# Fifth attention of a graph network: more weighing on the scalar engine, the norms' scalings moved to other passes, and the last two node tiles normalised one by one

## The chip, the cores and the metric

The kernel runs on one core of a Trainium2 chip. The core has a matrix engine (TensorE, PE), a vector engine (VectorE, DVE), a scalar engine (ScalarE, ACT), a general engine (GpSimd, POOL) and a queue that only issues transfers (SyncE, SP). [...]

The metric is the device time of one launch in microseconds (us), the median of several runs. The profile is one further execution, recorded by the hardware; its span runs from the first to the last instruction.

## The reference, cut to what matters

Four layers work on x, 8 batches x 2048 nodes x 64 features, over one graph. Each layer ends in `x = layernorm(x + layer(x))`. The change touches the last attention of the last layer (the fifth attention of the whole) and what follows it:

```python
def _gat_layer(h, mask, b):
    scores = jnp.einsum('...nd,...md->...nm', h, h)
    scores = jnp.where(mask, scores, NEG)
    attn = jax.nn.softmax(scores, axis=-1)
    return jnp.einsum('...nm,...md->...nd', attn, h) + b
...
out2 = _gat_layer(h2, mask[None], bo)
z2 = jax.nn.leaky_relu(out2, negative_slope=0.2)
mu = jnp.mean(z2, axis=-1, keepdims=True)
var = jnp.mean(jnp.square(z2 - mu), axis=-1, keepdims=True)
out = (z2 - mu) * jax.lax.rsqrt(var + LN_EPS) * gamma + beta
...
x = _layernorm(x + out, axis=-1)
```

So after the attention each node gets: a leaky ReLU, a first normalisation, a product with gamma, the addition of x (beta is already in x), and a second normalisation, which gives the result.

## The kernel before

The graph is sparse, so the kernel doesn't compute all scores. The 2048 nodes are 16 node tiles of 128. The edges of a node tile lie in 3 slots x 4 groups; a **unit** is one slot and two groups, so a node tile has 6 units (`PER`), and the stage has 96. Node tiles are treated in pairs, of 12 units.

For one unit the steps are:

- `fetch`: POOL starts two gathers, which bring the rows of the neighbours (`hs`, 128 edges x 8 batches x 64 features, twice) from a table in memory. Nine such buffers; units are fetched five passes ahead.
- `expand`: PE copies each node's own row to its edges (`pe`), by six matrix products with `selTb`, a 0/1 matrix in bf16.
- `score`: DVE multiplies `pe` and `hs` (`pr`, L1155) and sums over the features (`sc`, L1160); ACT takes the exponential into `w` (L1162), and for two units of three once more into `w_ps` in PSUM (L1164).
- `weigh_act` and `weigh`: the row of each edge is multiplied by its weight (`wx`). Of three units, POOL does the first whole (128x1024, L1176), ACT (eight activations of 128x64, L1171) and DVE (128x512, L1176) do half each of the second, and DVE does the third whole (128x1024, L1176). DVE reads the weights from `w_ps`.
- `add_up`: PE sums the weighed rows and the weights into the nodes (`po` L1188, `pd` L1190), with `self_`, a 0/1 matrix.

For one node tile follow `invert` (DVE, the reciprocal of `pd`, L1193), `divide` (ACT, eight activations, L1199), `leaky` (DVE, L1202), `take_stats` (DVE: `bn_stats` L137, then twelve small operations, L140 to L143, among them three Newton steps for the inverse root), `normalise` (ACT, eight activations, L151), `residual` (POOL: product with gamma L1215, addition of x L1216), again `take_stats`, and `store` (ACT scales, SP stores). `take_stats` does both tiles of a pair in one chain. `start` (SP and ACT) brings `hi` and makes `selTb` and `self_` for the next node tile.

The order is written out by hand (`manual_schedule`): one loop over passes u. Pass u does, in this order: fetch of unit u+5; score of unit u+1 (with `invert` between its product and its sum where a tile has ended); `weigh_act` of u-1; expand of u+2; `weigh` of u-1; add_up of u-2; then the work of whole tiles that a dictionary `after` gives by its offset; and, where u % 6 is 3, `start` of the next tile. An entry at offset j falls into the pass whose number, within its pair of twelve, is (j + 11) modulo 12. So before the change: `divide` of the first tile in pass 9 and its `leaky` in 10; `divide` of the second in 3, its `leaky` and the pair's statistics in 4; scalings in 6 and 7; gamma and x on POOL in 7 and 8; second statistics in 9; last scalings and stores in 10 and 0. `start` is in 3 and 9.

The buffers that matter: `pe` 2, `hs` 9, `wx` 4, `w` 5, `z` 6. The tile `w_ps` is one PSUM tile, and a read of any part of it waits for the last write to any part.

Of the kernel before, what the change touches and what calls it, by code (L numbers as in the profile page):

```python
# [27 lines left out]
AF = mybir.ActivationFunctionType  # L28
ALU = mybir.AluOpType
# [19 lines left out]
def kernel(ctx: ExitStack, tc: tile.TileContext, ins: dict, out: bass.AP):  # L49
    nc = tc.nc  # L50
    x, adj = ins["x"], ins["adj"]
    B, N, D = x.shape
    NT = N // P
# [26 lines left out]
    def rows(name, src, pool):  # L80

        n = src.shape[0]
        t = pool.tile([P, n], F32, name=name)
        nc.sync.dma_start(t, src.unsqueeze(0).to_broadcast([P, n]))
        return t

    def over(v, shape):

        for _ in shape[1:-1]:
            v = v.unsqueeze(1)  # L90
        return v.to_broadcast(shape)

    def along(v):

        return v.unsqueeze(len(v.shape)).to_broadcast([*v.shape, D])
# [25 lines left out]
    def inv_sqrt(y, v, t):  # L121

        nc.vector.scalar_tensor_tensor(y.bitcast(I32), v.bitcast(I32), -0.5, guess.to_broadcast(v.shape),
                                       op0=ALU.mult, op1=ALU.add)
        for _ in range(3):
            nc.vector.tensor_tensor(t, y, y, ALU.mult)
            nc.vector.scalar_tensor_tensor(t, t, -0.5, v, op0=ALU.mult, op1=ALU.mult)
            nc.vector.scalar_tensor_tensor(y, t, 1.5, y, op0=ALU.add, op1=ALU.mult)

    def norm_stats(chunks):  # L130

        n = len(chunks)
        st = small.tile([P, n, NP, 6], F32, name=f"st{n}")

        for c, v in enumerate(chunks):
            for a in range(NP):
                nc.vector.bn_stats(st[:, c, a], v[:, 2 * a:2 * a + 2, :].rearrange("p b d -> p d b"))  # L137
        triples = st.rearrange("p n a (k m) -> p (n a k) m", m=3)
        var, rstd, tmp, nmr = (small.tile([P, n * B], F32, name=f"ln_{k}{n}") for k in "vrtm")
        nc.vector.scalar_tensor_tensor(var, triples[:, :, 2], 1.0 / D, eps.to_broadcast(var.shape),  # L140
                                       op0=ALU.mult, op1=ALU.add)
        inv_sqrt(rstd, var, tmp)
        nc.vector.scalar_tensor_tensor(nmr, triples[:, :, 1], -1.0, rstd, op0=ALU.mult, op1=ALU.mult)  # L143
        return rstd, nmr

    def normed(chunks, stats):
        rstd, nmr = stats
        for c, v in enumerate(chunks):
            for b in range(B):
                k = c * B + b  # L150
                nc.scalar.activation(v[:, b], v[:, b], AF.Identity, scale=rstd[:, k:k + 1], bias=nmr[:, k:k + 1])  # L151
# [10 lines left out]
    X = main.tile([P, NT, B, D], F32, name="X")  # L162
# [97 lines left out]
    def node_products(t0, wk, ps):  # L260
# [26 lines left out]
        for q, ph in enumerate(held):  # L287
# [26 lines left out]
                                   op0=ALU.is_equal, op1=ALU.mult)  # L314
# [8 lines left out]
    for it in range(NT):  # L323
# [18 lines left out]
        for k in range(0, SL, 8):  # L342
            nc.vector.max(nbr[:, k:k + 8], topf)
            if k + 8 < SL:
# [19 lines left out]
                                       op0=ALU.is_le, op1=ALU.mult, saturate=False)  # L364
# [27 lines left out]
    held, zs, stats = {}, {}, {}  # L392
# [28 lines left out]
    def weigh(it):  # L421
        hs, self_, w, wm = held[it]
        po = ps_o.tile([P, BD], F32, name="po")
        pd = ps_w.tile([P, NG, B], F32, name="pd")
        for s in range(GS):
            own = slice(s * NG, (s + 1) * NG)
            wx = hs[:, own].rearrange("p g b d -> p (g b) d")
            nc.vector.tensor_tensor(wx, wx, along(w[:, own].rearrange("p g b -> p (g b)")), ALU.mult)  # L428
            nc.tensor.matmul(pd, self_[:, s], wm[:, own], start=(s == 0), stop=(s == GS - 1))
            for g in range(NG):  # L430
                nodes = slice(g * GN, (g + 1) * GN)
                nc.tensor.matmul(po[nodes], self_[:, s, nodes], hs[:, s * NG + g].rearrange("p b d -> p (b d)"),
                                 start=(s == 0), stop=(s == GS - 1))
        held[it] = po, pd
# [66 lines left out]
    with ExitStack() as l1:  # L501
# [115 lines left out]
        n = 0  # L617
# [94 lines left out]
    with ExitStack() as l2:  # L712
# [65 lines left out]
        def take_stats(st, k, v):  # L778
            for a in range(NP):
                nc.vector.bn_stats(st[:, k, a], v[:, 2 * a:2 * a + 2, :].rearrange("p b d -> p d b"))  # L780
# [76 lines left out]
        with tc.manual_schedule(engines=engines):  # L857
# [4 lines left out]
            n = 0  # L862
# [37 lines left out]
    with early, ExitStack() as heads:  # L900
# [6 lines left out]
        Us, os, xss, xsTs, ws, pos, h2s, zs, dTs = ({} for _ in range(9))  # L907
# [172 lines left out]
        with tc.manual_schedule(engines=engines):  # L1080
# [8 lines left out]
            for k in range(len(steps)):  # L1089
# [4 lines left out]
                it = steps[k][0]  # L1094
# [11 lines left out]
    with ExitStack() as fifth:  # L1106
# [10 lines left out]
        g3 = rows("g3", ins["L3_gnn_gamma"], fp)  # L1117
# [16 lines left out]
        units = [(it, s, g) for it in range(NT) for s in range(GS) for g in range(0, NG, 2)]  # L1134
        hss, pes, ws, wxs, zs, stats, sums = ({} for _ in range(7))
# [30 lines left out]

        def weigh_act(u):
            wxs[u] = fk.tile([P, 2, B, D], F32, name="wx", bufs=4)
            if u % 3 == 1:
                for b in range(B):  # L1170
                    nc.scalar.activation(wxs[u][:, 0, b], hss[u][:, 0, b], AF.Copy, scale=ws[u][:, 0, b:b + 1])  # L1171

        def weigh(u):
            eng, w = (nc.vector, w_ps[:, u % 3]) if u % 3 else (nc.gpsimd, ws[u])
            ks = slice(1, 2) if u % 3 == 1 else slice(0, 2)
            eng.tensor_tensor(wxs[u][:, ks].rearrange("p k b d -> p (k b) d"),  # L1176
                              hss[u][:, ks].rearrange("p k b d -> p (k b) d"),
                              along(w[:, ks].rearrange("p k b -> p (k b)")), ALU.mult)
# [23 lines left out]
            nc.vector.scalar_tensor_tensor(zs[it], zs[it], 0.2, zs[it], op0=ALU.mult, op1=ALU.max)  # L1202


        def take_stats(it):
            stats[it] = norm_stats([zs[it], zs[it + 1]])

        def normalise(it):
            rstd, nmr = stats[it - it % 2]
            own = slice(it % 2 * B, it % 2 * B + B)  # L1210
            normed([zs[it]], (rstd[:, own], nmr[:, own]))

        def residual(it):
            z = zs[it]
            nc.gpsimd.tensor_tensor(z, z, over(g3, z.shape), ALU.mult)  # L1215
            nc.gpsimd.tensor_tensor(z, z, X[:, it], ALU.add)  # L1216

        def store(it):
            normalise(it)
            nc.sync.dma_start(out[:, it * P:(it + 1) * P, :].rearrange("b p d -> p b d"), zs[it])  # L1220
# [1 line left out]


        after = {-2: [(divide, 0)], -1: [(leaky, 0)], 4: [(divide, 1)], 5: [(leaky, 1), (take_stats, 0)],
                 7: [(normalise, 0)], 8: [(residual, 0), (normalise, 1)], 9: [(residual, 1)], 10: [(take_stats, 0)],
                 11: [(store, 0)], 13: [(store, 1)]}
        PER = GS * NG // 2
        AHEAD = 5
        last = len(units) - 1
        with tc.manual_schedule(engines=engines):  # L1230
            for u in range(AHEAD):
                fetch(u)
            start(0)
            expand(0)
            expand(1)
            score(0, [])
            for u in range(len(units) + 14):
                if u + AHEAD <= last:
                    fetch(u + AHEAD)
                done, r = divmod(u - 2, PER)  # L1240
                ended = [(invert, done - 1)] if r == 0 and 1 <= done <= NT else []
                if u + 1 <= last:
                    score(u + 1, ended)
                else:
                    for f, a in ended:
                        f(a)
                if 1 <= u <= last + 1:
                    weigh_act(u - 1)
                if u + 2 <= last:
                    expand(u + 2)  # L1250
                if 1 <= u <= last + 1:
                    weigh(u - 1)
                if 2 <= u <= last + 2:
                    add_up(u - 2)
                for j, fs in after.items():
                    for k in (u - j - 2 * PER + 1,):
                        if k % (2 * PER) == 0 and 0 <= k < len(units):
                            for f, n in fs:
                                f(k // PER + n)
                if u % PER == 3 and u // PER + 1 < NT:  # L1260
                    start(u // PER + 1)

# [29 lines left out]
    with tc.If(bad > 0), ExitStack() as anyway:  # L1292
# [12 lines left out]
        X = main.tile([P, NT, B, D], F32, name="X")  # L1305
# [13 lines left out]
        with tc.tile_pool(name="adjp", bufs=3) as ap_, tc.tile_pool(name="adjps", bufs=4, space=PSUM) as aps:  # L1319
            for it in range(NT):  # L1320
# [15 lines left out]
                own = ap_.tile([P, P], F32, name="own")  # L1336
# [8 lines left out]
            for c in range(NCH):  # L1345
                pr = aps.tile([1, TPC, P], F32, name="pt")
                for k in range(TPC):
                    it = c * TPC + k
# [32 lines left out]
        with ExitStack() as l0:  # L1381
# [71 lines left out]
            for b in range(B):  # L1453
                p, k = divmod(b, 2)
# [8 lines left out]
                for ih in range(2):  # L1463
                    acc = [pa.tile([P, CW], F32, name="acc") for _ in range(2)]
                    for jt in range(NT):
                        w = pp.tile([P, HW], F32, name="w")
                        nc.vector.tensor_scalar(w, F[:, ih * HW:(ih + 1) * HW], Cj[:, jt, b:b + 1], Aj[:, jt, b:b + 1],
                                                op0=ALU.mult, op1=ALU.max)
                        nc.vector.scalar_tensor_tensor(w, MT[:, jt, ih * HW:(ih + 1) * HW], 0.0, w,
                                                       op0=ALU.is_equal, op1=ALU.mult)  # L1470
# [11 lines left out]
                if k == 1:  # L1482
                    for c in range(NCH):
# [6 lines left out]
                        v = wk.tile([P, TPC, P], F32, name="v", tag="t2")  # L1490
# [17 lines left out]
        with ExitStack() as l1:  # L1508
# [15 lines left out]
            for t in range(NT):  # L1524
# [7 lines left out]
                for h in range(2):  # L1532
                    hs = slice(h * HB * D, (h + 1) * HB * D)
                    f = R[:, t, h, 1]
# [99 lines left out]
        with ExitStack() as l3:  # L1634
# [44 lines left out]
            bias = wp.tile([D, HN + 1], F32, name="bias")  # L1679
# [3 lines left out]
            g3 = rows("g3", ins["L3_gnn_gamma"], wp)  # L1683
# [107 lines left out]
            units = [(b, h) for b in range(B) for h in range(HN + 1)]  # L1791
# [37 lines left out]
```

## Time and profile before

| what | value |
|---|---|
| timed runs, median of 3 | 2254.24 us (2251.59 to 2255.79) |
| profiled execution, its own time | 2154.42 us |
| span of the profiled execution | 2152.5 us |
| mean granted TensorE clock over the span | 0.791 |
| granted TensorE clock in the fifth attention | 0.50 |
| fifth attention, first gather to the end of the span | 1720.3 to 2152.5 us |
| busy in the span: PE, DVE, ACT, POOL | 1554.6, 1413.8, 992.9, 1068.2 us |

The profiled execution took 100 us less than the timed median. Times inside the kernel come from the profiled execution.

A line of the timeline has the start in us from the start of the span, the duration in us, the engine, the line of the code, the operation, what it writes and reads, how many instructions are merged, and in brackets the idle time before it with what ended it. A line of the windows has the stretch, its length, and for each engine the busy time and (in brackets) the number of instructions; then TensorE's granted clock, the mean busy share of the DMA engines, and GB/s. `DMA_INDIRECT` on POOL is the issue of one gather, not its transfer.

### The profile page before, as it was taken

The numbers are of one execution on the slowest core, as the hardware profiler recorded it, in microseconds if no ns is written. First come the engines' busy times: TensorE is split into PE (matmuls) and PEld (weight loads), VectorE is DVE, ScalarE is ACT, GpSimd is POOL, SyncE is SP. The second block draws the span as 40 slices with busy tenths as digits, with TensorE's granted clock in tenths as the row PEclk, the third lists the DMA queues.
The fourth block names the chain that finished last, engine by engine and source line by source line (L and its number), as shares of the span: only waits on it lengthen the run. The fifth ranks groups of instructions, "written<-read, shape, count | busy, mean of one in ns | idle before, by whom it ended". The sixth has DMA issues, their size and how long they took to land.

```text
span 2152.5 us, 35828 instructions
## 1 busy us (share of the span) xinstructions
PE 1554.6 (72%) x13538; PEld 879.8 (41%) x13574; DVE 1413.8 (66%) x2986; ACT 992.9 (46%) x2336; POOL 1068.2 (50%) x992
## 2 busy tenths in 40 slices
PE   3662445434899979475599998998999578888872
PEld 3552112111333354121477777777777422222210
DVE  6888488885655574445345555555555379999995
ACT  4552134448523242636445444444444235555555
POOL 0000777734645446342345455455454387777662
PEclk9965566656999999788699999999999655555555
DMA  6321666631278725443323233233233065555540
GB/s 195 132 98 63 208 204 206 206 101 60 99 270 294 256 69 155 129 122 93 108 71 110 83 98 110 84 98 109 85 99 92 34 200 153 160 159 156 156 125 21
DMA packets 134244, 283.70 MB, mean 132 GB/s; under 512 B 64144, under 2 KB 66704, under 8 KB 131984
## 3 DMA queue, kind: packets, MB, share of 16 engines
q0 software_dynamic: 64896, 217.10, 33.3%
q1 hardware_dynamic: 52528, 60.03, 8.4%
q10 hardware_dynamic: 16640, 4.20, 0.9%
q8 instruction: 109, 1.79, 0.3%
q14 instruction: 71, 0.58, 0.1%
HBM read 245.35 MB, written 35.91 MB: 131 GB/s over the span
## 4 chain that ended last, share of the span: by engine, by line
PE 35%; DVE 18%; ACT 10%; issue 5%; POOL 2%; DMA 2%; SPq 1%; ACTq 0%; POOLq 0%; DVEq 0%
PE pscore L968 9%; PE pa L556 6%; DVE w L977 4%; PE pa L867 3%; ACT w L971 3%; PE pm L1030 3%; PE po L994 3%; PE pt L953 2%; DVE pr L1155 2%; ACT z L786 2%; PE pm L920 2%; PE pa L608 2%; PE po L1188 2%; ACT z L151 2%; DVE sc L1160 2%
## 5 line engine op out<-in xcount | busy, mean ns | idle before, releaser
L977 DVE SCALAR_TENSOR_TENSOR w<-w,Sel 128x512 f32<-128x512 f32 (+1 forms) x192 | 178.9, 959 | 234.8 <-ACT w L971 234.2
L186 POOL DMA_INDIRECT hs<-htab,src x192 | 183.7, 957 | 267.2 <-PE pe L408 206.0
L186 POOL DMA_INDIRECT xs<-xtab,src x192 | 205.4, 1070 | 123.0 <-issue 93.6
L556 PE MATMUL pa<-R,ET 128*128 128x512 bf16 x841 | 196.5, 388 | 52.9 <-POOL R L544 34.0
L186 POOL DMA_INDIRECT hs<-ktab,src x192 | 186.3, 971 | 54.9 <-issue 42.1
L971 ACT ACTIVATE w<-pscore 128x1024 f32<-128x1024 f32 x128 | 131.0, 1023 | 164.3 <-PE pscore L968 163.7
L968 PE MATMUL pscore<-U,xsT 64*128 64x64 f32 (+1 forms) x3072 | 203.6, 280 | 3.3 <-DVE U L931 3.3
L968 PEld LDWEIGHTS pscore<-U,xsT 64*128 64x128 f32 x3072 | 184.0, 190 | 29.0 <-issue 21.5
L1038 POOL TENSOR_TENSOR h<-h,h2h 128x512 f32<-128x512 f32 x48 | 60.9, 1269 | 250.1 <-DVE h2h L1032 250.1
L955 ACT COPY xsT<-pt 128x512 f32<-128x512 f32 x192 | 112.1, 584 | 141.4 <-PE pt L953 141.4
L1150 PE MATMUL pe<-hi,selTb 32*128 32x512 bf16 x576 | 138.8, 619 | 50.5 <-DVE pr L1155 30.3
L151 ACT ACTIVATE X<-X,ln_m,ln_r 128x64 f32<-128x64 f32 x256 | 87.2, 428 | 172.0 <-DVE ln_m L143 172.0
L556 PEld LDWEIGHTS <-ET 128*128 128x128 fp8e4 x864 | 84.1, 99 | 174.2 <-issue 82.5
L994 PE MATMUL po<-w,xs 128*64 128x64 f32 (+1 forms) x3072 | 143.8, 243 | 2.0 <-DVE w L977 1.8
L953 PE MATMUL pt<-ident,xs 128*128 128x128 f32 x768 | 128.1, 290 | 8.0 <-DMA xs<-xtab,src 5.4
L994 PEld LDWEIGHTS po<-w,xs 128*64 128x64 f32 x3072 | 119.5, 137 | 34.9 <-issue 29.3
L1155 DVE TENSOR_TENSOR pr<-pe,hs 128x1024 f32<-128x1024 f32 x96 | 116.8, 1217 | 14.4 <-DMA hs<-ktab,src 10.5
L186 POOL DMA_INDIRECT rs<-ytab,src x84 | 80.7, 961 | 83.6 <-PE pa L847 60.5
L1160 DVE TENSOR_REDUCE sc<-pr 128x16 f32<-128x1024 f32 x96 | 117.1, 1220 | 2.9
L1162 ACT ACTIVATE w<-sc,shift 128x16 f32<-128x16 f32 x96 | 29.3, 305 | 191.3 <-DVE sc L1160 187.3
L186 POOL DMA_INDIRECT rs<-rtab,src x84 | 79.6, 948 | 72.9 <-PE pa L608 52.8
L428 DVE TENSOR_TENSOR hs<-hs,w 128x2048 f32<-128x2048 f32 x48 | 106.7, 2277 | 0.5 <-ACT w L418 0.5
(577 smaller groups left out, 3307.9 us busy)
## 6 DMA issues: line engine op xcount, KB each, us to landing
at<-in_adj SPq DMA_DIRECT2D x16, 1024.0 KB
rtab<-r SPq DMA_DIRECT2D x16, 512.0 KB
ptab<-hp SPq DMA_DIRECT2D x16, 384.0 KB
hi<-ptab SPq DMA_DIRECT2D x16, 384.0 KB
X<-in_x ACTq DMA_DIRECT2D x16, 256.0 KB
htab<-H SPq DMA_DIRECT2D x16, 256.0 KB
ytab<-y SPq DMA_DIRECT2D x16, 256.0 KB
ktab<-hb SPq DMA_DIRECT2D x16, 256.0 KB
```

What stands on the lines that cost most here:

```text
L151: nc.scalar.activation(v[:, b], v[:, b], AF.Identity, scale=rstd[:, k:k + 1], bias=nmr[:, k:k + 1])
L186: nc.gpsimd.indirect_dma_start(out=dst, out_offset=None, in_=table[:, :], in_offset=bass.IndirectOffsetOnAxis(ap=src[:, it, s, g:g + 1], a ...
L556: nc.tensor.matmul(po[h].rearrange("p a f -> p (a f)"), ET[:, jt, it * P:(it + 1) * P], R[:, jt, q, h].rearrange("p a f -> p (a f)"), star ...
L953: nc.tensor.transpose(pt[:, p], xss[k][n][:, p * P:(p + 1) * P], ident)
L955: nc.scalar.copy(xsT, pt)
L968: nc.tensor.matmul(pscore[:, k_, f0:f0 + HN * ni].rearrange("p (h i) -> p h i", i=ni), xsTs[k][t][half, p], Us[it][half, p, :, i0:i0 + ni] ...
L971: nc.scalar.activation(w.rearrange("p t k a h i -> p k t (a h i)"), pscore.rearrange("p k (t m) -> p k t m", t=n), AF.Exp)
L977: nc.vector.scalar_tensor_tensor(wt, wt, 3.0e38, edge, op0=ALU.min, op1=ALU.mult)
L994: nc.tensor.matmul(po[half, p, :, i0:i0 + ni], xss[k][t][:, f0:f0 + D], ws[k][:, t, k_, p], start=(s == 0 and p == 0), stop=(last and p == ...
L1150: nc.tensor.matmul(pe[:, k].rearrange("p b d -> p (b d)"), selTb[nodes, s * P:(s + 1) * P], hi[nodes, q], start=(q == 0), stop=(q == 2))
L1155: nc.vector.tensor_tensor(pr.rearrange("p k b d -> p (k b d)"), pes[u].rearrange("p k b d -> p (k b d)"), hss[u].rearrange("p k b d -> p ( ...
L1160: nc.vector.tensor_reduce(sc, pr, AX.X, ALU.add)
```

## The change

Five things are altered.

- ACT now does half of the weighing of the third unit of three as well, and DVE the other half. DVE has no whole weighing left.
- The entries of `after` move. First scalings: passes 7 and 10 (before: 6 and 7). Gamma and x of the first tile: pass 8; gamma of the second: pass 11; x of the second and the second statistics: pass 0 (before: statistics in 9). Last scalings and stores: passes 1 and 4 (before: 10 and 0).
- Adding x is on DVE for the second tile of each pair, on POOL for the first.
- The last two node tiles (14 and 15) don't go through `after`, but through a second dictionary, `alone`, with statistics of one tile each; their offset j is counted from the last unit of the tile itself, so that tile 14 has `divide` and `leaky` in pass 92, statistics and scaling in 93, gamma, x and second statistics in 94, and the store in 95; tile 15 the same in 98 to 101. Their scalings are shared, four batches on ACT and four on DVE, and gamma and x are on DVE.
- The loop ends seven passes earlier.

In a pass, entries of `after` come before those of `alone`.

```diff
         def weigh_act(u):
             wxs[u] = fk.tile([P, 2, B, D], F32, name="wx", bufs=4)
-            if u % 3 == 1:
+            if u % 3:
                 for b in range(B):
                     nc.scalar.activation(wxs[u][:, 0, b], hss[u][:, 0, b], AF.Copy, scale=ws[u][:, 0, b:b + 1])
 
         def weigh(u):
             eng, w = (nc.vector, w_ps[:, u % 3]) if u % 3 else (nc.gpsimd, ws[u])
-            ks = slice(1, 2) if u % 3 == 1 else slice(0, 2)
+            ks = slice(1, 2) if u % 3 else slice(0, 2)
...
+        PAIRED = NT - 2
+
         def take_stats(it):
-            stats[it] = norm_stats([zs[it], zs[it + 1]])
+            stats[it] = norm_stats([zs[it], zs[it + 1]] if it < PAIRED else [zs[it]])
 
         def normalise(it):
-            rstd, nmr = stats[it - it % 2]
-            own = slice(it % 2 * B, it % 2 * B + B)
-            normed([zs[it]], (rstd[:, own], nmr[:, own]))
-
-        def residual(it):
+            if it < PAIRED:
+                rstd, nmr = stats[it - it % 2]
+                own = slice(it % 2 * B, it % 2 * B + B)
+                normed([zs[it]], (rstd[:, own], nmr[:, own]))
+                return
+            rstd, nmr = stats[it]
+            for b in range(B):
+                v, r, n = zs[it][:, b], rstd[:, b:b + 1], nmr[:, b:b + 1]
+                if b % 2:
+                    nc.scalar.activation(v, v, AF.Identity, scale=r, bias=n)
+                else:
+                    nc.vector.tensor_scalar(v, v, r, n, op0=ALU.mult, op1=ALU.add)
+
+        def with_gamma(it):
             z = zs[it]
-            nc.gpsimd.tensor_tensor(z, z, over(g3, z.shape), ALU.mult)
-            nc.gpsimd.tensor_tensor(z, z, X[:, it], ALU.add)
+            eng = nc.gpsimd if it < PAIRED else nc.vector
+            eng.tensor_tensor(z, z, over(g3, z.shape), ALU.mult)
+
+        def with_x(it):
+            z = zs[it]
+            eng = nc.vector if it % 2 or it >= PAIRED else nc.gpsimd
+            eng.tensor_tensor(z, z, X[:, it], ALU.add)
...
         after = {-2: [(divide, 0)], -1: [(leaky, 0)], 4: [(divide, 1)], 5: [(leaky, 1), (take_stats, 0)],
-                 7: [(normalise, 0)], 8: [(residual, 0), (normalise, 1)], 9: [(residual, 1)], 10: [(take_stats, 0)],
-                 11: [(store, 0)], 13: [(store, 1)]}
+                 8: [(normalise, 0)], 9: [(with_gamma, 0), (with_x, 0)], 11: [(normalise, 1)], 12: [(with_gamma, 1)],
+                 13: [(with_x, 1), (take_stats, 0)], 14: [(store, 0)], 17: [(store, 1)]}
+
+        alone = {3: [divide, leaky], 4: [take_stats, normalise], 5: [with_gamma, with_x, take_stats], 6: [store]}
...
-            for u in range(len(units) + 14):
+            for u in range(len(units) + 7):
...
                 for j, fs in after.items():
-                    for k in (u - j - 2 * PER + 1,):
-                        if k % (2 * PER) == 0 and 0 <= k < len(units):
-                            for f, n in fs:
-                                f(k // PER + n)
+                    k = u - j - 2 * PER + 1
+                    if k % (2 * PER) == 0 and 0 <= k < PAIRED * PER:
+                        for f, n in fs:
+                            f(k // PER + n)
+                for j, fs in alone.items():
+                    k = u - j - PER + 1
+                    if k % PER == 0 and PAIRED * PER <= k < len(units):
+                        for f in fs:
+                            f(k // PER)
```

## The prediction

> **What bounds the kernel now.** I read, in this order: the page (engines, 40 slices), the windows of the fifth attention, its groups of instructions by form, the timeline of one period, and the timeline of the end. The fifth attention runs from about 1720 us to the end of the span. It repeats every two node tiles, that is every 12 passes of the loop; passes and units are counted from 0 within a pair (in the end: from the start of the stage), and pass u scores unit u+1, weighs u-1 and expands u+2:
>
> ```profile
> core 0: us, PE busy (x) PEld busy (x) DVE busy (x) ACT busy (x) POOL busy (x), PEclk, DMA share, GB/s
> 1852.99:1903.16 50.17, 40.31 (x170) 10.53 (x168) 46.61 (x77) 28.15 (x105) 36.05 (x33) 0.50 0.54 153
> 1903.16:1953.31 50.15, 40.32 (x170) 10.52 (x168) 46.59 (x78) 28.16 (x105) 36.03 (x33) 0.50 0.54 152
> ```
>
> The windows run from one reciprocal (L1193) to the same one a pair later. DVE works 46.6 of 50.15 us; ACT looks free for 22. What the engines do around pass 9 of a pair:
>
> ```profile
> 1857.62 0.26 ACT L1164 ACTIVATE w_ps<-sc,shift 128x16 f32<-128x16 f32 x1
> 1857.82 1.72 ACT L1199 ACTIVATE z<-po,recs 128x64 f32<-128x64 f32 x8
> 1857.91 1.22 DVE L1176 TENSOR_TENSOR wx<-hs,w_ps 128x1024 f32<-128x1024 f32 x1 [0.60 <-ACT w_ps L1164]
> ...
> 1859.39 0.56 ACT L1128 ACTIVATE selTb<-SelT 128x384 bf16<-128x384 fp8e4 x1
> ...
> 1860.01 1.46 PE L1150 MATMUL pe<-hi,selTb 32*128 32x512 bf16 x6 [0.63 <-ACT selTb L1128]
> ...
> 1862.71 0.96 POOL L186 DMA_INDIRECT hs<-ktab,src  x1 [0.30 <-issue]
> ...
> 1863.04 2.59 DVE L143 SCALAR_TENSOR_TENSOR ln_m<-st,ln_r 128x16 f32<-128x16 f32 x1
> ...
> 1863.68 1.91 POOL L1176 TENSOR_TENSOR wx<-hs,w 128x1024 f32<-128x1024 f32 x1
> 1865.56 1.21 DVE L1155 TENSOR_TENSOR pr<-pe,hs 128x1024 f32<-128x1024 f32 x1
> ...
> 1871.40 2.00 ACT L1171 ACTIVATE wx<-hs,w 128x64 f32<-128x64 f32 x8
> ```
>
> Three things to see. PE gets selTb only after ACT's eight divisions; DVE doesn't feel it, because it is in the statistics of this place. L143 takes 2.59 us where its twin at 1892.34 takes 0.17, and ends with POOL's weighing. And DVE waits 0.60 for w_ps.
>
> Spacings on DVE, from the same timeline: product to sum 1.25, sum to next 1.14, half weighing 0.60, whole weighing 1.14, a weighing behind w_ps 0.68 later. Three units are 3 x 2.39 + 0.60 + 0.68 + 1.14 = 9.58. A pair: 4 x 9.58 + two leaky at 0.60 + two statistics at 4.15 + the stretched L143 2.41 = 50.2, the period. So DVE's order is the bound, and PE (3.32 a unit, 40) is next.
>
> [...] The trace agrees: L143, and one leaky of 1.61 us (median 0.68) that ends 0.56 after POOL's weighing. [...] 332 ns with one pointer, 426 with two, eight in 2.00 us, so the next starts after 1.91.
>
> **The change part by part, for a pair.**
> *Weighing.* DVE's four whole weighings become halves: -4 x 0.54 = -2.2. ACT gets 4 x 8 activations, 1.91 us each time, behind w_ps and ahead of what else is queued in that pass. In passes 3 and 9 these are the divisions, then selTb and self_. So leaky in passes 4 and 10 waits: in pass 4 before, the divisions ended at 1885.79 and leaky began at 1887.69; now 1887.70 against 1887.14. +0.6 in pass 4.
> *Passes 9 to 11.* From w_ps (0.29 ahead of the weighing of unit 8): weighing by ACT at 0.20, divisions 1.91 later, selTb 1.57 later, 0.56 for it, 0.06 to PE, 1.50 until the product may start: product 0 at 5.5 after that weighing. DVE would be there after 0.60 + 1.25 + 1.14 + 0.60 = 3.6: +1.9 (0.6 of it in front of leaky). Before, 6.5 us of statistics lay here; they move to pass 0. PE's next expansion comes 1.39 + 1.92 = 3.31 later, DVE's 2.99: +0.3.
> *Adding x.* One of two on DVE: +0.6 at leaky's spacing (128x512, both inputs in SBUF). POOL loses 1.3, and isn't the bound.
> *Statistics moved.* The old collision goes: -2.41. Is there a new one? Count from the sum of unit 8. ACT: exp 1.32 later, 0.21 and 0.20, eight scalings 2.75, end at 4.5. POOL waits there with gamma for tile 0, then, at spacings of the trace: gamma +0.08, x 1.35, four gathers 1.42 + 1.30 + 1.26 + 1.27, weighing 0.97, gathers 2.07 + 1.30, gamma 0.98, gathers 1.41 + 1.30 + 1.26 + 1.27, weighing of unit 0 after 0.97: at 22.7, to 24.6. [...] DVE: to the weighing of unit 8 7.2, product 0 at 12.7, product 1 at 16.0, then 1.25 + 1.82 + 0.60 + adding x 0.60 + eight bn_stats 1.69: the twelve small operations (2.5 in all) begin at 22.0. So they meet POOL's weighing at their first or second, wait until 24.6, and ten are left, 2.1: +2.2 (2.6 if all twelve wait). Bounds: 0 if they miss it, 2.6.
> Scalings in other units: ACT's longest row now (scalings, exp, eight weighings) ends 0.2 before the exp of unit 4 is due; nothing added. SP's stores now alternate with hi; hi leaves behind unit 11's expansion, 4 us ahead of selTb: nothing.
> Sum: 50.15 - 2.2 + 0.6 + 1.9 + 0.3 + 0.6 - 2.4 + 2.2 = 51.2, some +1.1 a pair (1.2 unrounded). Six pairs between passes 20 and 92: +7. Before pass 20, where PE is the bound and only selTb's delay shows: +0.7.
>
> **The end.** Product 93 starts at 2102.54, the span ends 50.0 later. After, from that product: ACT has scalings until 3.3, exp, eight weighings until 5.4, divisions of tile 14 until 7.1; leaky 14 stands directly behind in DVE's queue, ahead of product 94, and waits for them and for POOL's weighing of unit 93 (end 7.9): done 8.5. Product and sum 94, weighing, statistics (four bn_stats 0.85, twelve small 2.5) 15.4; four tensor_scalar 128x64 aren't in the trace: [...] 15.9. Sum 95 at 17.2, gamma and x 1.4, second statistics with 1.2 lost to POOL's gamma: 24.2. Two weighings, scalings, x and the paired statistics: 30.7. ACT then scales tile 12 first, 33.4, and divides tile 15, 35.1. Leaky 35.9, statistics 39.2, scalings on both engines 40.7, gamma and x 42.2, statistics 45.5, scalings 47.0, last store 4.4 (as before): 51.4. Normalising the last tile alone shortens what follows its leaky from 26.0 (2126.5 to 2152.5) to 15.5, but the stalls ahead eat it: +1.4 (-4 to +5).
>
> Together 7 + 0.7 + 1.4 = +9, with the unrounded +1.2 9.5: profiled execution 2154.42 to 2164. The timed median, 2254.24, is 100 us above the profiled execution; I assume that lies in stages where TensorE's granted clock is above the 0.50 of this one, so the same difference holds: 2263.7.
>
> **Rivals.** *Cover holds:* ACT's idle 22 us really take the weighings, and the new place meets no POOL weighing. Then DVE's own sum, 50.15 - 2.2 + 0.6 - 2.4 = 46.2, -3.9 a pair, six pairs and the end's -1: 2230. For it: the busy shares. Against: the fixed queue order. It decides if selTb comes within 3.6 us of the weighing of unit 8 and leaky finds its divisions done. *Collision missed:* the small operations pass POOL by 2.6 us on either side; 6 x 2.2 less: 2250. My two paths meet within 0.1, so an error of 0.5 doesn't miss. *Second collision:* leaky of pass 10 starts 0.6 ahead of POOL's weighing of unit 9; if it is late it waits 2.6, of which the next collision gives half back: +1 to +2 a pair, 2270 to 2276.
>
> **How the numbers follow.** Forecast 0.53 (own range 2256 to 2271), cover holds 0.17, collision missed 0.15, second collision 0.15. A measurement of this kernel tells about 0.2% (4.5 us) from no change. Slower: forecast and second collision, less a little, 0.66; same: most of collision missed and the edge of the forecast, 0.15; faster 0.19. Range 2247 to 2275: it leaves out cover holds and a rest.
>
> **What would show it.** In the new profile: period 51.2; DVE's product 0 of each pair waiting more than 1 us for PE, which waits for selTb; leaky waiting for ACT's divisions; L140 or L123 stretched beyond 2 us, L143 at 0.17; leaky 14 waiting some 4 us. A period under 49, a product 0 without wait, or no stretched small operation would prove me wrong.

## The result and the profile after

The changed kernel took 2264.57 us (median of 6 runs, 2260.22 to 2269.09), the kernel before, timed beside it, 2254.74 (6 runs, 2251.22 to 2256.64). The ratio is 1.0048, with a 95% interval of 1.0031 to 1.0065: slower by some 10 us (by the interval 7 to 15).

The profiled execution of after took 2262.87 us, its span 2260.9; that of before had 2152.5. Most of this difference is not the change's: the reciprocal in pass 8, the first with which the two can be compared, comes at 1758.34 in before and at 1854.82 in after, 96 us later, ahead of all that was altered. From there to the end of the span before needs 394.1 us and after 406.1, so the stage itself got 12.0 us longer. Of these 1.3 lie between the reciprocals of passes 8 and 20, 8.6 in the six pairs from 20 to 92, and 2.1 behind 92.

The windows of after, from one reciprocal (L1193) to the same one a pair later (the columns are those of the windows shown for before):

```profile
core 0: us, PE busy (x) PEld busy (x) DVE busy (x) ACT busy (x) POOL busy (x), PEclk, DMA share, GB/s
1900.62:1952.14 51.52, 39.82 (x170) 10.51 (x168) 45.45 (x79) 35.57 (x137) 34.79 (x31) 0.53 0.52 148
1952.14:2003.65 51.51, 39.71 (x170) 10.47 (x168) 45.45 (x78) 35.55 (x137) 34.79 (x31) 0.53 0.52 149
```

DVE's busy time fell by 1.2 us, and yet the pair became 1.35 longer (51.51 against 50.16, the mean of the two). So DVE stands idle 6.1 us in a pair where it was 3.6 before. The timeline of after, from pass 9 of a pair to pass 1 of the next, shows where:

```profile
1956.94 2.01 ACT L1171 ACTIVATE wx<-hs,w 128x64 f32<-128x64 f32 x8
...
1958.85 1.70 ACT L1199 ACTIVATE z<-po,recs 128x64 f32<-128x64 f32 x8
...
1960.42 0.54 ACT L1128 ACTIVATE selTb<-SelT 128x384 bf16<-128x384 fp8e4 x1
1960.58 0.69 DVE L1202 SCALAR_TENSOR_TENSOR z<-z 128x512 f32<-128x512 f32 x1 [0.47 <-issue]
...
1961.01 1.46 PE L1150 MATMUL pe<-hi,selTb 32*128 32x512 bf16 x6 [2.34 <-DVE sc L1160]
...
1962.51 1.22 DVE L1155 TENSOR_TENSOR pr<-pe,hs 128x1024 f32<-128x1024 f32 x1 [1.24 <-PE pe L1150]
...
1965.83 1.23 DVE L1155 TENSOR_TENSOR pr<-pe,hs 128x1024 f32<-128x1024 f32 x1 [0.24 <-PE pe L1150]
...
1971.83 0.18 DVE L140 SCALAR_TENSOR_TENSOR ln_v<-st,eps 128x16 f32<-128x16 f32 x1
1972.04 2.61 DVE L123 SCALAR_TENSOR_TENSOR ln_r<-ln_v,guess 128x16 int32<-128x16 int32 x1
...
1972.69 1.91 POOL L1176 TENSOR_TENSOR wx<-hs,w 128x1024 f32<-128x1024 f32 x1
...
1976.56 0.18 DVE L143 SCALAR_TENSOR_TENSOR ln_m<-st,ln_r 128x16 f32<-128x16 f32 x1
```

ACT's row is the cause: eight weighings, then eight divisions, then selTb. The leaky waits 0.47 for the divisions; the brackets say "issue", but it starts 0.03 after they end. PE starts 0.05 after selTb (done at 1960.96), although its bracket names a sum on DVE, which had ended 0.90 before. Product 0 then waits 1.24 for PE, product 1 another 0.24. The stretched small operation has moved from L143 in pass 9 to L123 in pass 0; it again begins 0.65 ahead of the recorded start of POOL's weighing (0.64 in before) and ends with it, and L143 takes 0.18. (Of the twelve small operations, L140 is the first and L143 the last; the ten between them, the first guess of the inverse root and its Newton steps, stand in lines L123 to L128.)

The timeline of after in the end of the stage, from pass 92 to the second statistics of tile 14:

```profile
2212.29 2.00 ACT L1171 ACTIVATE wx<-hs,w 128x64 f32<-128x64 f32 x8
...
2214.20 1.69 ACT L1199 ACTIVATE z<-po,recs 128x64 f32<-128x64 f32 x8
...
2214.84 1.90 POOL L1176 TENSOR_TENSOR wx<-hs,w 128x1024 f32<-128x1024 f32 x1
2215.92 1.36 DVE L1202 SCALAR_TENSOR_TENSOR z<-z 128x512 f32<-128x512 f32 x1 [4.01 <-ACT z L1199]
2217.20 1.21 DVE L1155 TENSOR_TENSOR pr<-pe,hs 128x1024 f32<-128x1024 f32 x1
...
2224.20 0.98 DVE L1222 TENSOR_SCALAR z<-z,ln_r,ln_m 128x64 f32<-128x64 f32 x4
...
2230.92 1.26 POOL L1227 TENSOR_TENSOR z<-z,g 128x512 f32<-128x512 f32 x1 [14.19 <-ACT z L151]
2231.05 1.16 DVE L127 SCALAR_TENSOR_TENSOR ln_t<-ln_t,ln_v 128x8 f32<-128x8 f32 x1
```

Leaky 14 holds DVE for 4.01 us and product 94 stands behind it. It takes 1.36 instead of 0.68, while POOL is weighing unit 93 (until 2216.74), and a small operation takes 1.16 instead of 0.17 beside POOL's gamma.

### The profile page after: what moved, and what is told of

Same layout as the page of the kernel before. It is cut to its first block, busy times and chain, and to the rows that moved or that the text cites. A ratio compares the mean times of both kernels' runs of the same rounds, so it can differ in the third digit from the quotient of the medians.

```text
span 2260.9 us, 36109 instructions
## 1 busy us (share of the span) xinstructions
PE 1609.5 (71%) x13538; PEld 912.0 (40%) x13574; DVE 1419.2 (63%) x3037; ACT 1047.6 (46%) x2576; POOL 1052.6 (47%) x981
## 4 chain that ended last, share of the span: by engine, by line
PE 37%; DVE 16%; ACT 11%; issue 5%; another core or an unknown queue 3%; POOL 2%; DMA 1%; SPq 1%; ACTq 0%; DVEq 0%; POOLq 0%
PE pscore L968 7%; PE pa L556 6%; PE po L994 4%; PE pt L953 3%; PE pm L920 3%; PE pa L867 3%; PE pm L1030 3%; DVE pr L1155 3%; DVE w L977 2%; ACT w L971 2%; ACT z L786 2%; DVE sc L1160 2%; PE pa L608 2%; ACT wx L1171 2%
## 5 line engine op out<-in xcount | busy, mean ns | idle before, releaser
L968 PE MATMUL pscore<-U,xsT 64*128 64x64 f32 (+1 forms) x3072 | 224.9, 285 | 21.6 <-issue 15.0
L968 PEld LDWEIGHTS pscore<-U,xsT 64*128 64x128 f32 x3072 | 198.4, 195 | 52.9 <-issue 42.5
L994 PE MATMUL po<-w,xs 128*64 128x64 f32 (+1 forms) x3072 | 158.1, 255 | 3.1 <-DVE w L977 1.8
L994 PEld LDWEIGHTS po<-w,xs 128*64 128x64 f32 x3072 | 131.3, 145 | 40.5 <-issue 34.5
L953 PE MATMUL pt<-ident,xs 128*128 128x128 f32 x768 | 134.1, 300 | 13.1 <-ACT xsT L955 7.7
L1171 ACT ACTIVATE wx<-hs,w 128x64 f32<-128x64 f32 x512 | 128.2, 333 | 0.0
```

The source lines that it names most:

```text
L953: nc.tensor.transpose(pt[:, p], xss[k][n][:, p * P:(p + 1) * P], ident)
L968: nc.tensor.matmul(pscore[:, k_, f0:f0 + HN * ni].rearrange("p (h i) -> p h i", i=ni), xsTs[k][t][half, p], Us[it][half, p, :, i0:i0 + ni] ...
L994: nc.tensor.matmul(po[half, p, :, i0:i0 + ni], xss[k][t][:, f0:f0 + D], ws[k][:, t, k_, p], start=(s == 0 and p == 0), stop=(last and p == ...
```

## The experiments

Ten kernels were run, in three jobs on different chips, where the kernel before had medians of 2254.21, 2240.50 and 2152.63 us. As with the two profiles above, that difference lies ahead of the fifth attention. So kernels are compared by their ratio to before in the same job, and, in the profiled executions, by the stage from the reciprocal of pass 8 to the end of the span, which doesn't contain it. All of them in one table (us, from the timelines; the ratio with its 95% interval):

| kernel | passes 8 to 20 | 20 to 92 (six pairs) | 92 to end | all, against before | ratio of the medians |
|---|---|---|---|---|---|
| before | 44.5 | 300.8 | 48.8 | 0 | 1 |
| after | 45.8 | 309.4 | 50.9 | +12.0 | 1.0048 (1.0031 to 1.0065) |
| weigh_only | 45.8 | 299.3 | 51.0 | +1.9 | 1.0008 (1.0001 to 1.0015) |
| order_only | 44.5 | 304.3 | 52.3 | +7.0 | 1.0034 (1.0019 to 1.0050) |
| stats_later | 45.9 | 296.4 | 50.9 | -1.0 | 0.9997 (0.9986 to 1.0007) |
| divide_first | 44.7 | 299.8 | 50.9 | +1.3 | 1.0002 (0.9989 to 1.0015) |
| both_moved | 44.7 | 293.2 | 51.0 | -5.3 | 0.9969 (0.9957 to 0.9981) |
| stats_two_later | 44.8 | 291.9 | 55.0 | -2.5 | 0.9994 (0.9975 to 1.0012) |
| tail_leaky | 45.9 | 308.4 | 47.6 | +7.7 | 1.0033 (1.0015 to 1.0051) |
| lone_only | 44.5 | 300.9 | 50.5 | +1.8 | 1.0013 (0.9998 to 1.0028) |
| moved_and_tail | 44.2 | 293.0 | 47.6 | -9.3 | 0.9971 (0.9959 to 0.9983) |
| two_later_and_tail | 44.2 | 291.7 | 47.6 | -10.6 | 0.9961 (0.9948 to 0.9975) |

Each stage is from one profile. Up to pass 92 tail_leaky has the code of after, and yet its six pairs are 1.1 us shorter (the reason is shown with that kernel); both_moved and moved_and_tail, also the same up to there, differ by 0.5 ahead of pass 20. So a difference of about 1 us in the column "all" says little by itself.

The stage and the ratio agree for every kernel within the interval, but for moved_and_tail, where the stage says 9.3 us less and the interval ends at 8.8 (0.0041 of 2152.63).

**weigh_only.** The kernel before with the new weighing alone.

```diff
-            if u % 3 == 1:
+            if u % 3:
...
-            ks = slice(1, 2) if u % 3 == 1 else slice(0, 2)
+            ks = slice(1, 2) if u % 3 else slice(0, 2)
```

> The kernel before with nothing but the new weighing (ACT does half of the third unit too, DVE the other half). Theory 1, the place in the queues: the cost of the change lies in the moved order, not in the weighing. In the old order the statistics of pass 9 cover selTb and leaky of pass 10, and POOL's gamma starts 1.9 us later because ACT's scalings do, so that DVE's small operations are over before POOL's weighing begins. Per pair -2.2 for DVE, +0.6 for leaky of pass 4, +1.1 for a late exp in pass 9, -2.4 for the collision: period 47.2, time about 2237. Theory 2, ACT's load: the weighing on ACT is itself the loss, because eight activations stand in front of what others wait for: period 50.2 or more, time 2254 or more.

The medians were 2254.73 us against 2254.21 of before, and the first periods 49.46, 49.45 and 50.04 us. The median is what theory 2 had (2254 or more), but the period is neither theory's (47.2, or 50.2 and more). The timeline of its pass 9 and 10:

```profile
1955.49 2.01 ACT L1171 ACTIVATE wx<-hs,w 128x64 f32<-128x64 f32 x8
1955.58 0.69 DVE L1176 TENSOR_TENSOR wx<-hs,w_ps 128x512 f32<-128x512 f32 x1 [1.66 <-ACT w_ps L1164]
...
1957.81 0.88 DVE L137 BATCH_NORM_STATS2 st<-z 128x6 f32<-128x128 f32 x4 [0.75 <-POOL z L1216]
...
1962.71 1.91 POOL L1176 TENSOR_TENSOR wx<-hs,w 128x1024 f32<-128x1024 f32 x1
...
1963.53 1.66 DVE L1202 SCALAR_TENSOR_TENSOR z<-z 128x512 f32<-128x512 f32 x1
```

DVE is here earlier by the halves it no longer has to weigh, and meets three things that were hidden: the weights w_ps, which come 1.0 later because ACT now has scalings directly behind its weighings; x from POOL, 0.75; and, with the small operations done ahead of POOL's weighing, the leaky now falls into it and takes 1.66 instead of 0.68. In the end DVE waits 7.06 us for PE at the last reciprocal, where it was 4.91 before. So of the 2.0 us a pair only 0.7 are kept in each of the three shortest pairs, and 1.6 in all six together; the passes before 20 lose 1.3 and the end 2.2. In every pair the product of pass 3 waits too, 0.72 us in three pairs and 1.13 to 2.13 in the other three; what ends this wait the profile names as PE's sum `pd`, which the product doesn't read, or not at all, so its cause is open.

**order_only.** The changed kernel with the old weighing: the diff of weigh_only the other way round.

> The changed kernel with the old weighing (DVE does the third unit whole). Theory 1: no wait for selTb (it comes 0.5 us before DVE needs it) and none in front of leaky, but DVE has its 2.2 us back and the small operations still meet POOL's weighing of unit 0, after five or six of them: period about 51.0, time 2260 to 2263. Theory 2: without the weighing on ACT the new order gains the old collision and pays the added x: 50.15 - 2.4 + 0.6 = 48.4, time about 2244.

The median was 2260.9 us (2254.21 before), the period 50.67 in most pairs: theory 1 (2260 to 2263, about 51.0). The collision is only exchanged: in pass 0, L128, the eighth small operation, takes 2.48, and L143 is free. What is left is x on DVE, 0.5 a pair by the period. Product 0 and leaky do not wait. So those waits come from the weighing in front of the divisions. The new order, with x on DVE and the lone tiles, by itself costs 3.5 us in the six pairs and 3.5 in the end. The two halves of the change don't add: in the six pairs the weighing alone gains 1.6 us and the order alone loses 3.5, which makes +1.9, but together they lose 8.6. The weighing that pays a little in the old order costs 5.1 in the new one, where the statistics of pass 9 no longer stand between it and product 0 (in weigh_only they do, and product 0 doesn't wait).

**stats_later.** The changed kernel, with the second statistics and the first store of a pair one pass later.

```diff
-                 13: [(with_x, 1), (take_stats, 0)], 14: [(store, 0)], 17: [(store, 1)]}
+                 13: [(with_x, 1)], 14: [(take_stats, 0), (store, 0)], 17: [(store, 1)]}
```

> The changed kernel with the second statistics of each pair one pass later (pass 1, ahead of the store there). Adding x stays in pass 0. Theory 1, [...] the small operations begin only 0.8 us before it ends; the stretched operation shrinks to about 1 us. Period 51.5 - 2.0 = 49.5, time about 2252. Rival, no collision: L123 is long because of something of its own place (what precedes it on DVE), so it stays long wherever the statistics are: period 51.5, time 2264.

The period is 49.35, 2.17 us less than after, and the median 2253.08 (2254.21 before): the collision is worth what was put down for it. (The 0.8 of theory 1 counts to the end of POOL's weighing of unit 0.) The timeline of stats_later where the small operations now meet POOL's weighing of unit 0:

```profile
1972.02 1.65 DVE L137 BATCH_NORM_STATS2 st<-z 128x6 f32<-128x128 f32 x8
1972.19 1.91 POOL L1176 TENSOR_TENSOR wx<-hs,w 128x1024 f32<-128x1024 f32 x1
...
1973.71 0.43 DVE L140 SCALAR_TENSOR_TENSOR ln_v<-st,eps 128x16 f32<-128x16 f32 x1
```

The eight bn_stats run beside POOL's weighing at their usual length (1.65, against 1.66 in pass 4); only the first small operation is caught by its tail, and takes 0.43 instead of 0.18. Why the one is held and the other isn't, no run here shows.

**divide_first.** The changed kernel, with ACT's divisions, selTb and self_ ahead of the eight weighings in passes 3 and 9, for all but the last two tiles.

```diff
-            if u % 3:
+            if u % 3 and not late(u):
+                act_half(u)
+
+        def late(u):
+            return u % PER == 2 and u < PAIRED * PER
+
+        def act_half(u):
                 for b in range(B):
...
                     start(u // PER + 1)
+                if u and late(u - 1):
+                    act_half(u - 1)
```

> The changed kernel with ACT's eight weighings of passes 3 and 9 put behind the divisions, selTb and self_ of the same pass. Both theories: no wait in front of leaky, and product 0 no longer waits for selTb. Theory 1a, the end of the collision is set by POOL: DVE arrives 1.1 earlier at the small operations, does five more of them ahead of POOL's weighing and then waits for its end as before, so only about 0.5 + 0.6 of the 2.4 us of waits is gained: period 50.4, time about 2258. Theory 1b, waits add up: all of 2 x 0.47 + 1.24 + 0.24 is gained: period 49.1, time about 2250.

The period is 49.82 and the median 2254.23 (2254.21 before), between the two. The timeline from the leaky of pass 10 to pass 1 (lines are six higher in this kernel):

```profile
2010.86 0.68 DVE L1208 SCALAR_TENSOR_TENSOR z<-z 128x512 f32<-128x512 f32 x1
...
2012.26 1.93 PE L1194 MATMUL po<-wx,self__16336 128*32 128x512 f32 x4 [0.83 <-ACT wx L1177]
...
2015.69 1.22 DVE L1155 TENSOR_TENSOR pr<-pe,hs 128x1024 f32<-128x1024 f32 x1 [1.15 <-PE pe L1150]
...
2022.94 2.46 DVE L127 SCALAR_TENSOR_TENSOR ln_t<-ln_t,ln_v 128x16 f32<-128x16 f32 x1
2023.43 1.92 POOL L1182 TENSOR_TENSOR wx<-hs,w 128x1024 f32<-128x1024 f32 x1
2025.43 0.17 DVE L128 SCALAR_TENSOR_TENSOR ln_r<-ln_t,ln_r 128x16 f32<-128x16 f32 x1
```

The leaky no longer waits, nor does product 0; but PE waits 0.83 for ACT's late half, and product 1 waits 1.15 for PE. What DVE gains besides goes into the collision: POOL's weighing starts where it did, and DVE has run seven small operations when it comes (the last of them held), where after had run two. In this half of the pair 1.13 us are gained, 1.05 of them by those five. The other half gained 0.57.

**both_moved.** stats_later and divide_first together.

> Changed kernel with two moves at once: the second statistics and the first tile's store of a pair one pass later (in pass 1), and in passes 3 and 9 ACT's divisions and selTb ahead of ACT's eight weighings. Alone the moves gave 2.17 and 1.70 us a pair. Theory 1 (the small operations are held by POOL's weighing of unit 0, wherever DVE's path comes to lie): the second move brings DVE some 2.1 us earlier to this place, so that the small operations, which just missed POOL's weighing when the statistics alone were moved, are held again, L140 or L123 for over 2 us; of the second move only its other half, 0.6, is left: period 48.6 to 48.9, 2247 to 2250. Theory 2 (gains add): 51.5 - 2.2 - 1.7 = 47.6 or, with the five operations that the second move had lost, 46.9: 2236 to 2241, and no small operation beyond 0.5 us.

The period is 48.71 and the ratio 0.9969, which is 2247 us on the scale of the first job: theory 1. Each move gains 2.17 and 1.70 alone, and both together 2.81. The timeline, where the small operations meet POOL:

```profile
1911.81 1.91 POOL L1182 TENSOR_TENSOR wx<-hs,w 128x1024 f32<-128x1024 f32 x1
1912.43 1.34 DVE L140 SCALAR_TENSOR_TENSOR ln_v<-st,eps 128x16 f32<-128x16 f32 x1
```

L140 is held for 1.34, not for over 2 as theory 1 had it, since DVE comes only 1.0 us earlier than in stats_later (21.10 instead of 22.08 behind the reciprocal of pass 8): product 1 waits for PE here too (1.14). The end of the hold hasn't moved. Counted from the reciprocal of pass 8, POOL's weighing starts 20.55 later in after, 20.56 in stats_later and 20.48 in both_moved.

**stats_two_later.** As both_moved, with the second statistics one pass later again.

```diff
-                 13: [(with_x, 1)], 14: [(take_stats, 0), (store, 0)], 17: [(store, 1)]}
+                 13: [(with_x, 1)], 15: [(take_stats, 0), (store, 0)], 17: [(store, 1)]}
```

> As both_moved, but the second statistics and the first tile's store two passes later (in pass 2), clear of POOL's weighing of unit 0. Theory 1 (held operations and ACT's order are all that cost time): no small operation beyond 0.3 us, no wait of leaky for ACT's divisions, DVE's own sum again: period 46.7 to 47.3, 2234 to 2240. Theory 2 (behind DVE another bound stands, PE's expansions waiting for rows or for ACT's late halves): 48.0 or more, 2245 and above, with a product that waits over 1 us for PE in each half of a pair.

No small operation is stretched, and yet the period is 48.5 and the ratio 0.9994. Theory 2 was nearer, though a product waits over 1 us for PE in one half of the pair only. The timeline of its DVE has, beside a product that waits 1.14 for PE as in both_moved, this:

```profile
2012.45 0.21 DVE L1199 RECIPROCAL recs<-pd 128x8 f32<-128x8 f32 x1 [0.73 <-PE pd L1196]
```

PE is the next bound: DVE now reaches the reciprocal before PE has summed the tile. In the end the last pair's statistics stand in pass 98 with tile 15's work; its last leaky waits 4.49 for ACT's divisions there, against 2.08 in after, and the end takes 55.0.

**tail_leaky.** The changed kernel with the lone tiles' leaky behind the next product.

```diff
-        alone = {3: [divide, leaky], 4: [take_stats, normalise], 5: [with_gamma, with_x, take_stats], 6: [store]}
+        alone = {3: [divide], 4: [leaky, take_stats, normalise], 5: [with_gamma, with_x, take_stats], 6: [store]}
```

> Changed kernel with the leaky of the lone tiles one pass later (behind product 94 instead of ahead of it). Theory 1 (leaky 14 standing ahead of product 94 holds DVE for 4.0 us, and this is on the path to the end): leaky 14 waits under 0.5 us, product 94 starts some 4 us earlier, and the end from product 93 falls from 52.1 to 48 to 49: 2260.5 to 2261.5. Theory 2 (the stall only shows a wait that comes back at the next product or at ACT's divisions of tile 15): under 1.5 us gained, 2263 to 2264.5. Period 51.5 in both.

From product 93 (2195.09) to the end (2243.9) it takes 48.8 us, against 52.1: 3.3 gained. The ratio is 1.0033, 0.0015 below that of after; the two intervals overlap, so the gain is shown in the profile and not by the times alone. The timeline of tail_leaky:

```profile
1959.17 0.17 DVE L123 SCALAR_TENSOR_TENSOR ln_r<-ln_v,guess 128x16 int32<-128x16 int32 x1
1959.38 2.42 DVE L126 TENSOR_TENSOR ln_t<-ln_r 128x16 f32<-128x16 f32 x1
...
2198.08 1.22 DVE L1155 TENSOR_TENSOR pr<-pe,hs 128x1024 f32<-128x1024 f32 x1
...
2200.46 1.69 ACT L1199 ACTIVATE z<-po,recs 128x64 f32<-128x64 f32 x8
...
2202.55 0.69 DVE L1176 TENSOR_TENSOR wx<-hs,w_ps 128x512 f32<-128x512 f32 x1 [2.00 <-ACT w_ps L1164]
2203.15 0.69 DVE L1202 SCALAR_TENSOR_TENSOR z<-z 128x512 f32<-128x512 f32 x1
```

Product 94 no longer waits; of the 4.0 us the weighing behind it gives 1.4 back (w_ps is late by 2.00 instead of 0.62), and leaky, behind POOL's weighing, takes 0.69 instead of 1.36.

The first two lines show why its pairs are shorter than those of after (51.34 us against 51.51) though the code there is the same: here L123 went through and the operation behind it was held, to 1961.80. In after and divide_first the held operation ended 0.05 behind POOL's weighing of 1.91 and 1.92; so here the weighing is put, by estimate, at 1959.85, 0.68 after the start of L123; in after L123 started 0.65 ahead and was held itself. So DVE stands close to the edge of the hold, and between these two executions one small operation more got ahead of it.

**lone_only.** The kernel before with nothing but the last two tiles treated singly, so with the old entries in `after` and the old weighing.

```diff
+                 7: [(normalise, 0)], 8: [(with_gamma, 0), (with_x, 0), (normalise, 1)], 9: [(with_gamma, 1), (with_x, 1)],
+                 10: [(take_stats, 0)], 11: [(store, 0)], 13: [(store, 1)]}
...
+            eng = nc.gpsimd if it < PAIRED else nc.vector
             eng.tensor_tensor(z, z, X[:, it], ALU.add)
```

> Kernel before with nothing but the last two tiles normalised singly, as in the changed kernel. Theory 1 (the stall of leaky 14 and the statistics and scalings of tile 14, which come on DVE ahead of tile 15, eat what the shorter work behind the last leaky gives): the end from product 93 takes 50.0 to 53.5, 2254 to 2258, and leaky 14 waits about 4 us. Theory 2 (normalising singly by itself shortens the end, and only the new weighing and order lengthen it again): 44 to 48, 2248 to 2252. Period 50.15 in both.

The end from product 93 takes 51.6 us (2183.86 to 2235.5), 1.7 more than before, and leaky 14 waits 4.03: theory 1, in the profile. By the times (1.0013, 0.9998 to 1.0028) it may be nothing; a gain of 2 us or more, as theory 2 had it, is outside the interval.

**moved_and_tail** and **two_later_and_tail.** The first is both_moved with tail_leaky's line. The second moves the second statistics of all pairs but the last to pass 2:

```diff
-                 13: [(with_x, 1)], 14: [(take_stats, 0), (store, 0)], 17: [(store, 1)]}
+                 13: [(with_x, 1)], 14: [(settle_last, 0)], 15: [(settle, 0)], 17: [(store, 1)]}
```

`settle` is statistics and store for the other pairs, `settle_last` for the last one.

> both_moved and tail_leaky together. Theory 1 (the pair's collision and ACT's order, and the stall of leaky 14, are separate terms and their gains add): period 48.7, 33.3 us less in no place but these: six pairs at 2.8 and the end at 3.3, together some 20 us below the changed kernel and 10 below the kernel before, a ratio of 0.995 to 0.996. Theory 2 (in the end the shorter passes only meet the wait of PE or ACT sooner): the end's 3.3 are lost, a ratio of 0.997.

> As moved_and_tail, but every pair except the last paired one has its second statistics and first store in pass 2 instead of pass 1. In stats_two_later the period was 48.5, 0.2 under both_moved, and only its end was 4 us longer, where the last pair's statistics fell into the work of tile 15. Theory 1 (that is the only harm): five pairs at 0.2 under moved_and_tail, a ratio of 0.9945 to 0.996, and the end from the reciprocal of pass 92 takes 47.6 again. Theory 2 (PE's wait costs elsewhere too): 0.997 or more.

(The 33.3 in the first text is a slip and stands for nothing; the sum meant is the 20 that follows.) In the stage the gains add: 293.0 and 47.6 us in the first, 291.7 and 47.6 in the second, so that the first needs 21.2 less than the changed kernel, 384.9 instead of 406.1. The medians are 2144.65 and 2143.29 us, against 2152.63 of before: 0.9971 and 0.9961. For the first, the ratio taken alone is nearer to theory 2, though its interval reaches theory 1; the profile, where the end's 3.3 are there, speaks for theory 1. For the second, theory 1 had the end right (47.6), and the six pairs are 1.4 us shorter than in the first; its ratio lies between the two theories, and its interval reaches both. By the times, both_moved and these two can't be told from each other; all three are faster than both kernels of this case.

## Why the prediction was right

The forecast was 2263.7, and the measured 2264.57 came from the mechanisms it named. By its own steps, in us a pair (measured, as predicted, by DVE's spacings, from the start of one instruction to the start of the next, in the pairs from 1852.99 of before and from 1952.14 of after):

| step of the prediction | predicted | measured | shown by |
|---|---|---|---|
| DVE's four weighings halved | -2.2 | -2.04 | trace of after |
| leaky in pass 4 waits for the divisions | +0.6 | +0.55 | divide_first: gone |
| passes 9 to 11: leaky and product 0 behind selTb | +1.9 | +1.89 | divide_first, order_only: gone |
| product 1 | +0.3 | +0.32 | trace of after |
| x on DVE | +0.6 | +0.60 | trace of after; order_only: period +0.5 |
| old collision goes, new one comes | -2.4 + 2.2 | -0.04 | stats_later: 2.17 gained |
| all other spacings | 0 | +0.07 | trace of after only |
| sum | +1.0 | +1.35 | period 50.17 to 51.51 |

A wait costs a little more than its idle time: a DVE instruction that needn't wait starts up to 0.08 ahead of the end of the one before it (the sums are 1.22 long and the next starts after 1.14), and one that waits loses that. So the four waits behind ACT's row are 2.4 us of idle time and cost 2.8.

The new collision was the step with most room to fail, for it rests on two paths of over 20 us meeting. Both came as counted out: from the sum of unit 8, DVE's small operations begin at 22.0 (predicted 22.0) and POOL's weighing at 22.9 (22.7). In before, L143 was held although it started 0.64 ahead of POOL's recorded start; counted so, the hold was to begin by 22.1 (22.7 less 0.64). The weighing met the second small operation, and cost 2.44 (2.61 less the usual 0.17), 0.2 more than put down for it. The row of the table holds all 24 small operations of a pair.

The closeness of the total is luck. The prediction's printed terms add up to +1.0 a pair, not to the 1.1 or the "1.2 unrounded" with which it goes on; with 1.0, its own way of summing gives 6 + 0.7 + 1.4, or 2262. And the interval of the measurement is 8 us wide. What the runs bear out are the terms one by one, not the last microsecond.

Six pairs gave +8.6 (predicted 7), the passes ahead of 20 gave +1.3 (predicted 0.7; it comes from the weighing in front of the divisions, for weigh_only has it too and divide_first only 0.2), and the end +2.2 from product 93 (predicted 1.4). In the end the leaky's stall was right at 4.0. The term that was mis-sized is the scaling on DVE: the product behind the four tensor_scalar of tile 14 started 0.90 after the first of them, where the prediction had put 0.5 (15.4 to 15.9), a guess: no trace of before has this instruction. By the end of the paired statistics after was 0.4 behind the predicted times (31.1 us from product 93, predicted 30.7), and the last store took 4.6 instead of 4.4. All together the stage is 12.0 longer in the profiles, against 9.5 predicted and 9.8 between the medians.

That the profiled execution and the median differ only ahead of the stage was an assumption. The profiles bear it out: after's came 96 us later to the stage and its median is 10 us higher. What makes that difference, no run here shows; that it goes with the granted clock stays the author's assumption. "Cover holds" fell, because ACT's 22 free us lie behind its queue's order and not at the places where the leaky and PE wait. "Collision missed" is what stats_later does. The "second collision", the leaky of pass 10 with POOL's weighing of unit 9, doesn't happen in after, but it does in weigh_only.

Two things stay open: the product that waits in pass 3 of weigh_only, and whether treating the last tiles singly is a loss by the clock, since lone_only's interval reaches below 1.

## What to carry to other kernels

When work is moved to an engine with much idle time, look at what stands behind it in that engine's queue, not at the busy share: here 32 activations a pair fitted into 22 free us and still put 2.4 us of waits on DVE, because they were queued ahead of the divisions and of selTb. And when an instruction is stretched by another engine's hold, moving it can be worth nothing (0.04 us a pair in after) unless the new place is counted out from the same start on both engines; here the hold's end was set by POOL, whose weighing started 20.55, 20.56 and 20.48 us behind the reciprocal in after, stats_later and both_moved, and gains ahead of it vanished into it, as they did in divide_first and both_moved. With that removed, the next bound (here PE, 0.7 at the reciprocal) takes its share at once.

## What the runs showed of the hardware

- What stood behind a waiting instruction in DVE's queue waited with it: in after leaky 14 waited 4.01 us and product 94, next in the queue, started 8.37 us after product 93; in tail_leaky, with the leaky behind it, 2.99 us after.
- DVE's weighing of unit 8 reads its own part of `w_ps`, and started in before (1857.91) 0.60 us late, 0.03 after ACT had written the part of unit 10 (1857.62, 0.26 long).
- An activation of 128x64 took 332 ns on ACT with a scale from memory (the weighings of before) and 426 with a scale and a bias (its scalings); eight weighings in a row took 2.00 us.
- A small operation that is otherwise recorded at 0.17 us took 2.61 (L123 of after) beside a weighing on POOL that is recorded at 1.91, and ended with it. Operations were held that started well ahead of POOL's recorded start: by 0.65 us in after (L123 at 1972.04, POOL at 1972.69) and by 0.49 in divide_first. Those that started 0.70 ahead in divide_first and, by the estimate given there, 0.68 ahead in tail_leaky still took 0.17. Whether the hold begins early or POOL's start is recorded late, no run here shows.
- Four tensor_scalar of 128x64 with two scalars from memory took 0.98 us on DVE in after (L1222), and what followed started 0.90 after the first of them; the four activations that do the same work on ACT (L1220) took 1.43.
- The same kernel's medians on three chips lay 102 us apart (2254.21 to 2152.63), while in the profiles this stage took nearly the same time: a period of 48.71 in both_moved and of 48.69 in moved_and_tail, from the second and the third job.
